# Square roots moved to GpSimd as powers, and pivots as ratios of a recurrence, in a two-layer graph network with an eigenvector chain

## The chip, the cores and the metric

The kernel runs on one core of one Trainium2 chip. The time is device microseconds for one execution; before the change it is 2428.49 us, the median of three runs (2427.74 to 2430.24). TensorE (PE) multiplies matrices, VectorE (DVE), ScalarE (ACT) and GpSimd (POOL) do elementwise work, and SyncE (SP) issues the transfers. Each engine runs its own instructions in order.

## The reference

The input is `x`, 64 batches of 256 nodes with 256 features, in float32, and one adjacency matrix `adj` of 256 x 256. Two layers follow each other, each behind a layer norm with a relu and a residual add:

```python
h = jnp.maximum(_layernorm(x, axis=-1), 0.0)
x = x + _L0_gnn_ref(h, adj, adj, W1, W2, W3)    # three graph convolutions, widths 512, 1024, 256
h = jnp.maximum(_layernorm(x, axis=-1), 0.0)
x = x + _L1_gnn_ref(h, adj, W1, b1, W2, b2)     # in the eigenvectors of a Laplacian
```

Layer 0 multiplies by `adj * adj` and by a weight three times in turn. Layer 1 builds the normalized Laplacian of `adj`, takes all its eigenvectors `U` (`jnp.linalg.eigh`), and computes `U relu(U^T h W1 + b1) W2 + b2` with them. So `U` depends on `adj` alone, but layer 1 can't begin without it.

## The kernel before

Two pieces of work run beside each other. The **chain** (class `Eigen`) finds the eigenvectors; it is sequential and mostly VectorE's. The **products** of layer 0 (class `Layers`) are TensorE's, 32 pairs of batches, with ScalarE emptying the PSUM banks. When the chain has ended, layer 1 runs over the 32 pairs (`layer1`, line 2107).

The chain has four stages. `laplacian` (402) makes the degrees, their roots (`root`, 349: a ScalarE square root, then one Newton step on VectorE) and the matrix. `tridiagonalize` (439) takes 254 Householder steps. In each, `length` (483) makes the squared length `nn` of the column and its root `s0`; the sign `q`, the products `qn`, `qs` and the reciprocal `rs` of the root make `nb` (513); `ac` follows from it, TensorE turns `ac` into a row (`psB`), and from there the next column `xn` and the updates of `A` (559 to 561). Small operations are on GpSimd (`aside`, 470) while the row number is below 128, and on VectorE after that; `alpha` and `none` are always on GpSimd. `leaves` (959) then solves 16 blocks of 16 at once, each block on eight partitions: `all_parts` (819) makes 32 steps, each of them a sequence of 15 pivots, one after the other:

```python
for k in range(w1):
    at, nxt = slice(k, k + 1), slice(k + 1, k + 2)
    self.recip(r[:, at], (q if k else asig)[:, at])
    self.stt(q[:, nxt], r[:, at], nba[:, at], asig[:, nxt], OP.mult, OP.add)
```

Between the pivots it puts operations left over from the step before (`behind`, from `turn_vectors`). Meanwhile `reflections` (583) builds the orthogonal matrix with TensorE. Last, `level` (1280) joins the blocks in four levels, with `rational_steps` (1189) for the roots of the secular equation (ScalarE roots of `rdq`, 24 in all) and roots `zh` and `rn` for the vectors. A flag `bad` is set when some test fails; then `mend` (1726) joins again with slower, safer methods.

The order of TensorE and ScalarE is written out by the planner `Pace` (161), and VectorE's, GpSimd's and SyncE's by the framework. For each operation of the chain `Pace.chain` works out when its inputs are due, by costs that it holds itself (`Op`, 83), and puts operations of layer 0 in front of it until then (`run`, 227). Its costs for the chain are multiplied by 1.06, in the blocks of 16 by 1.13. Two streams give it this filler: `products` (1849) and `rows` (1872), which makes the layer norms (`norm`, 1811) ahead of layer 0 and of layer 1, 64 in all. The last pair's turned rows and its product for layer 1 (1868 to 1870) are held until layer 1 has reached pass LAST_AT - 1 - 3 = 8. When the chain has ended, 3.5 us of filler cover the flag's reading (FLAG_US) and 4.5 us the first loads (LOAD_US). In `layer1` the planner puts about one filler operation before each of its own; at pass 8 `pace.finish()` puts out all that is left of layer 0 in one piece. Layer 1 takes the pairs in the order 0 to 10, 30, 31, 11 to 29; the last two pairs' inputs stay in SBUF, the others go through DRAM.

All of these calls pass through two helper lines, so the profile shows them as L209 (the planner's `issue`) or L213 (past `pace.finish`); tiles tell them apart. Tile names have their numbers cut off: `s` is `s0`, `m` is `nb`, `m1` and other matrices, `q` stands for all small vectors of `all_parts`, `psB` is the row of `ac`, `c` the columns `c0` to `c6`, `bank` every PSUM bank of the layers.

Of the kernel before, what the change touches and what calls it, by code (L numbers as in the profile page):

```python
# [21 lines left out]
F32 = mybir.dt.float32  # L22
AF = mybir.ActivationFunctionType
OP = mybir.AluOpType
# [58 lines left out]
class Op:  # L83
# [4 lines left out]
    def __init__(self, part, call, args, kwargs):  # L88
        self.part, self.engine, self.call, self.args, self.kwargs = part, ENGINES[part], call, args, kwargs
        self.name = call.__name__  # L90
        free = lambda a: int(np.prod([int(n) for n in a.shape[1:]]))
        named = dict(kwargs)
        outs = [named.pop("out")] if "out" in named else [args[0]]
        ins = [a for a in [*(args if "out" in kwargs else args[1:]), *named.values()] if isinstance(a, bass.AP)]
        total = named.pop("accum_out", None)
        if isinstance(total, bass.AP):
            outs.append(total)
            ins = [a for a in ins if a is not total]
        self.outs, self.ins = [span(a) for a in outs], [span(a) for a in ins]
        n = max(free(a) for a in outs[:1] + ins) if self.engine == "DVE" else free(outs[0])  # L100
        sums = len(outs) > 1

        if self.engine == "PE":
            self.columns = 0 if "transpose" in self.name else n
            self.busy = max(n * self.COLUMN, 0.224) if self.columns else 0.115
            self.until = max(self.busy, 0.165) + 0.35
        elif self.engine == "ACT":
            pointers = any(isinstance(kwargs.get(k), bass.AP) for k in ("scale", "bias"))
            self.busy = 0.13 + n / 1400 + 0.12 * pointers + 0.19 * sums
            self.until = self.busy + 0.12  # L110
        elif self.engine == "DVE":
            each = 6.3 if self.name == "reciprocal" else 2.0 if self.name == "tensor_tensor_scan" else 1.0
            pointers = self.name == "scalar_tensor_tensor" or any(a.shape[1:] == [1] for a in ins[1:])
            self.busy = 0.065 + 0.06 * pointers + each * n / 960 + 0.08 * sums
            self.until = self.busy + 0.125
        elif self.engine == "POOL":
            self.busy = 0.2 + 2 * n / 960
            self.until = self.busy + 0.1
        else:
            self.busy, self.until = 0.1, 4.0  # L120
# [160 lines left out]
class Eigen:  # L281


    def __init__(self, tc, ctx, ap, gt2, pace):
# [10 lines left out]
        self.load_matrices(0, 1)  # L295
        self.iota, self.far, self.ones = (pool.tile([P, N], F32, name=c) for c in ("iota", "far", "ones"))
        tc.nc.vector.memset(self.ones, 1.0)

        self.nc.scalar.activation(self.far[:, 0:1], self.ones[:, 0:1], AF.Sqrt)
        self.cols = pool.tile([P, 1 + len(LEVELS), H], F32, name="cols")  # L300
# [44 lines left out]

    def recip(self, out, a):
        return self.nc.vector.reciprocal(out, a)

    def root(self, out, a, tmp, scale=1.0):

# [51 lines left out]
    def laplacian(self):  # L402
# [11 lines left out]
        self.tt(deg, deg, t, OP.add)  # L414
        self.tt(deg, deg, dg, OP.subtract)

        safe, rt, tmp = self.col("c3"), self.col("c4"), self.col("c5")
        self.ts(safe, deg, 1e-30, OP.max)
        self.root(rt, safe, tmp)
        dinv = self.col("c6")  # L420
        self.recip(dinv, rt)
# [17 lines left out]
    def tridiagonalize(self, a):  # L439
# [22 lines left out]
            return ps  # L462

        row = lambda tag: self.sp.tile([P, N], F32, tag=tag, name=tag)
        guard = self.col("guard", 1)
        nc.vector.memset(guard, 1e-30)
        book = self.mat("m1")
        alphas, nbs, tails = book[:, 0, :], book[:, 1, :], self.mat("m2")[:, 0, :]

# [12 lines left out]

        def length(xr, lo, tail):

            nn, s0, q, qn = (self.col(c, 1) for c in ("nn", "s0", "q", "qn"))
            x1 = xr[:, lo : lo + 1]
            self.stt(nn, x1, x1, tail, OP.mult, OP.add)
            nc.scalar.activation(s0, nn, AF.Sqrt, bias=guard)
            aside(lo).tensor_scalar(q, x1, 0.0, 0.5, OP.is_ge, OP.subtract)
            aside(lo).tensor_tensor(qn, q, nn, OP.mult)  # L490
            return nn, s0, q, qn
# [6 lines left out]
        nn, s0, q, qn = length(xr, 1, tail)  # L498
        for k in range(N - 2):
            lo = k + 1  # L500
            r, rest = slice(lo, N), slice(lo + 1, N)
# [1 line left out]
            hs = slice(halves[0], H)  # L503
            rc = a[:, :, lo]

            rs, qs, nb = self.col("rs", 1), self.col("qs", 1), nbs[:, k : k + 1]
            self.recip(rs, s0)
            aside(lo).tensor_tensor(qs, q, s0, OP.mult)
            xa, junk = self.col("xa"), self.row("r0")
            for h in halves:  # L510
                self.stt(junk[:, r], a[:, h, r], 1.0, xr[:, r], OP.mult, OP.mult, accum=xa[:, h : h + 1])
                if h == halves[0]:
                    self.stt(nb, rs, qn, qs, OP.mult, OP.add)

            ac, uc = self.col("ac"), us[:, :, k]
            self.stt(ac[:, hs], rc[:, hs], nb, xa[:, hs], OP.mult, OP.add)
# [44 lines left out]
                self.stt(a[:, h, r], xr[:, r], wc[:, h : h + 1], a[:, h, r], OP.mult, OP.add)  # L561
            xr, xc = xn, xcn
            if more:
                alpha, tail, (nn, s0, q, qn) = alpha1, tail1, following

        done = slice(0, N - 2)
        e0 = self.row("r1")[:, done]
# [120 lines left out]
    def vec(self, tag, w=LEAF):  # L688
        return self.lp.tile([P, w], F32, tag=tag, name=tag)
# [129 lines left out]
    def all_parts(self, d, bb, es, z, pend, bad):  # L819
# [21 lines left out]
        ad, thr, df, q4, rt, m, adh, sg, st, ebs, den, ba, nba, sgr, asig = (vec() for _ in range(15))  # L841
        q, r, qi, t, gs, qq, x, s2, p = (vec() for _ in range(9))

        def couplings():

# [36 lines left out]
        for step in range(QL_QUICK):  # L882
# [62 lines left out]
        put_aside()  # L945
        left = self.lp.tile([P, 1], F32, tag="ln", name="left", bufs=2)
        nc.vector.tensor_reduce(left, act, AX.X, OP.add)
        self.tt(bad, bad, left, OP.add)
        self.tt(t, d, d, OP.mult)
        self.ts(t, t, 4.0, OP.is_le)  # L950
# [238 lines left out]
    def rational_steps(self, n, kd, zsum, zown, znxt, acc, s, gap, half, y, bs, rb):  # L1189
# [33 lines left out]
        for step in range(ROOT_STEPS):  # L1223
# [41 lines left out]
            nc.scalar.activation(dq, dq, AF.Sqrt)  # L1265
            self.tt(b, b, dq, OP.add)
            self.recip(b, b)
            self.tt(g, g, b, OP.mult)
# [11 lines left out]
    def level(self, n, qt, dc, rho, sg, bad=None):  # L1280
# [392 lines left out]
        self.recip(zp, zp)  # L1673
        self.root(zh, zp, tmp)
# [13 lines left out]
        self.root(rn, nrm, tmp)  # L1688
        self.recip(rn, rn)
# [43 lines left out]
class Layers:  # L1733


    def __init__(self, tc, ctx, ap, gt2, u, ut):
# [21 lines left out]
        self.b2 = pool.tile([P, N], F32, name="b2")  # L1758
        self.u1 = pool.tile([P, H], F32, name="u1")
        self.ub2 = pool.tile([P, H, N], F32, name="ub2")  # L1760

    def load_weights(self):
        dma, ap = self.nc.sync.dma_start, self.ap
# [47 lines left out]
    def norm(self, x, scale, shift, parts=range(4)):  # L1811

        nc = self.nc
        g = H * 2
        at = slice(parts[0], parts[-1] + 1, parts[1] - parts[0])
        s, nm, v, tmp = (self.sp.tile([P, g], F32, tag=c, name=c) for c in ("s", "nm", "v", "tmp"))
        for j in parts:
            junk = self.sp.tile([P, N], F32, tag="junk", name="junk", bufs=1)
            yield nc.scalar.activation(junk, x[:, j // 2, j % 2, :], AF.Copy, accum_out=s[:, j : j + 1])
        yield nc.vector.tensor_scalar(nm[:, at], s[:, at], -1.0 / N, None, OP.mult)  # L1820
        for j in parts:
            junk = self.sp.tile([P, N], F32, tag="junk", name="junk", bufs=1)
            yield nc.scalar.activation(
                junk, x[:, j // 2, j % 2, :], AF.Square, bias=nm[:, j : j + 1], accum_out=v[:, j : j + 1]
            )
        s, nm, v, tmp, scale, shift = (t[:, at] for t in (s, nm, v, tmp, scale, shift))
# [371 lines left out]
```

## Time and profile before

| | |
|---|---|
| median of the runs | 2428.49 us |
| span of the profiled execution | 2426.6 us |
| TensorE busy | 2381.5 us |
| VectorE busy | 2127.2 us |
| ScalarE busy | 1013.8 us |
| GpSimd busy | 480.6 us |
| mean granted clock of TensorE | 0.999 |
| the chain: steps of the tridiagonal stage end | 1325 us |
| blocks of 16 end, levels begin (about) | 1766 us |
| flag written | 2243.2 us |
| layer 1's products alone | from 2293 us |

The profiled execution's own time is its span; the median of the runs, which also counts what lies around the span, is 1.9 us longer. "Busy" counts an engine's instructions, overlaps once. A row of a group gives the busy time, the mean ns of one and the idle time before it with its cause. Each float32 matmul or transpose of the program appears as two records.

### The profile page before, as it was taken

What the parts mean: (1) busy time and instruction counts of PE and PEld (TensorE: products, weight loads), DVE (VectorE), ACT (ScalarE), POOL (GpSimd) and SP (SyncE); (2) the same over time, 40 slices, a digit from 0 to 9 for tenths busy, and PEclk for the clock granted to TensorE, in tenths of its full rate; (3) what the DMA queues carried; (4) which work ended last, traced back from release to release, by engine and by line L of the source; (5) the groups of instructions that cost most, each with busy time, mean ns of one, the idle gap of its engine ahead of it and who ended that gap; (6) DMA issues with size and microseconds to landing.
All of it is one profiled execution on the core that took longest, in us unless ns stands there. A gap on an engine that the chain in (4) does not pass through costs nothing. (4 is left out here: it accounts for less than half of the span.)

```text
span 2426.6 us, 38393 instructions
## 1 busy us (share of the span) xinstructions
PE 2381.5 (98%) x9226; PEld 1581.7 (65%) x9226; DVE 2127.2 (88%) x12971; ACT 1013.8 (42%) x2827; POOL 480.6 (20%) x1752
## 2 busy tenths in 40 slices
PE   7999999999999999999999899999999999999999
PEld 4666666666666566666666666666566666666788
DVE  8999999999999999999999989999997888886443
ACT  4444454444444444344444244344344434443322
POOL 2334333343333111111111000000000000000443
PEclk9999999999999999999999999999999999999999
DMA  3000000000000000000000000000000000000676
GB/s 113 18 21 7 23 23 18 23 23 23 6 23 23 18 22 23 22 6 23 23 23 26 10 23 23 23 23 22 18 22 27 22 23 12 16 22 1 210 255 204
DMA packets 59399, 90.02 MB, mean 37 GB/s; under 512 B 5792, under 2 KB 42784, under 8 KB 59168
## 3 DMA queue, kind: packets, MB, share of 16 engines
q1 hardware_dynamic: 59168, 87.52, 10.8%
q8 instruction: 74, 1.21, 0.2%
q14 instruction: 157, 1.29, 0.2%
HBM read 47.13 MB, written 40.37 MB: 36 GB/s over the span
## 5 line engine op out<-in xcount | busy, mean ns | idle before, releaser
L209 PE MATMUL bank<-y,L_gnn_W 128*128 128x512 f32 (+2 forms) x2182 | 903.5, 566 | 1.1 <-ACT y L209 1.1
L209 PEld LDWEIGHTS bank<-y,L_gnn_W 128*128 128x128 f32 x2182 | 401.8, 190 | 440.7 <-issue 419.0
L209 PE MATMUL bank<-L_gnn_W,s 128*128 128x256 f32 (+1 forms) x2092 | 465.2, 375 | 3.2 <-ACT s L209 3.2
L209 PEld LDWEIGHTS bank<-L_gnn_W,s 128*128 128x128 f32 x2092 | 386.7, 190 | 52.2 <-ACT s L209 3.9
L209 ACT ACTIVATE s<-bank 128x512 f32<-128x512 f32 x384 | 224.9, 586 | 196.4 <-PE bank L209 196.0
L209 PE MATMUL bank<-gt,s 128*128 128x256 f32 x1036 | 233.7, 379 | 2.8 <-ACT s L209 2.8
L209 PE MATMUL bank<-L_gnn_W,y 128*128 128x512 f32 (+2 forms) x542 | 230.9, 569 | 1.1 <-ACT y L209 1.1
L209 PEld LDWEIGHTS bank<-gt,s 128*128 128x128 f32 x1036 | 194.7, 191 | 39.7 <-issue 10.5
L209 ACT COPY y<-bank 128x512 f32<-128x512 f32 x192 | 111.5, 582 | 138.9 <-PE bank L209 138.6
L209 PEld LDWEIGHTS bank<-L_gnn_W,y 128*128 128x128 f32 x542 | 100.2, 190 | 97.3 <-issue 91.1
L209 POOL COPY m<-xr 128x1 f32<-128x1 f32 x254 | 55.8, 220 | 534.5 <-DVE xr L209 526.5
L209 ACT ACTIVATE s<-nn,guard 128x1 f32<-128x1 f32 x254 | 74.5, 293 | 208.1 <-DVE nn L209 169.0
L209 ACT ACTIVATE h<-x,shift,scale 128x256 f32<-128x256 f32 x256 | 137.3, 589 | 54.6 <-DVE shift L209 54.4
L209 ACT ACTIVATE junk<-x 128x256 f32<-128x256 f32 x256 | 105.6, 412 | 95.8 <-DVE x L209 80.5
L209 ACT ACTIVATE junk<-x,nm 128x256 f32<-128x256 f32 x256 | 129.0, 504 | 37.1 <-DVE nm L209 32.6
L209 DVE SCALAR_TENSOR_TENSOR A<-xr,wc,A 128x255 f32<-128x255 f32 (+63 forms) x381 | 139.9, 368 | 0.0
L209 DVE SCALAR_TENSOR_TENSOR A<-wr,q,A 128x255 f32<-128x255 f32 (+63 forms) x381 | 138.9, 366 | 0.0
L209 ACT ACTIVATE junk<-xr 128x254 f32<-128x254 f32 (+63 forms) x127 | 46.0, 362 | 216.5 <-DVE xr L209 211.4
L209 DVE SCALAR_TENSOR_TENSOR q<-q 128x1 f32<-128x1 f32 (+1 forms) x576 | 119.8, 208 | 13.0 <-ACT q L209 2.3
L209 PE MATMUL bank<-gt,h 128*128 128x256 f32 (+1 forms) x518 | 120.6, 382 | 0.1
L209 POOL TENSOR_TENSOR xb<-x,ub 128x512 f32<-128x512 f32 x16 | 19.9, 1271 | 495.5 <-DMA hw<-hw 485.6
L209 PE MATMUL bank<-p,gt 128*128 128x512 f32 (+2 forms) x270 | 117.0, 570 | 0.1
(615 smaller groups left out, 4306.2 us busy)
## 6 DMA issues: line engine op xcount, KB each, us to landing
x<-x SPq DMA_DIRECT2D x60, 512.0 KB, 3.6
x<-in_x_dram SPq DMA_DIRECT2D x64, 256.0 KB, 3.7
out_dram<-out SPq DMA_DIRECT2D x64, 256.0 KB, 2.2
hw<-hw SPq DMA_DIRECT2D x60, 256.0 KB, 2.7
L_gnn_W<-in_L_gnn_W_dram SPq DMA_DIRECT2D x1, 2048.0 KB, 10.9
L_gnn_W<-in_L_gnn_W_dram SPq DMA_DIRECT2D x1, 1024.0 KB, 13.5
L_gnn_W<-in_L_gnn_W_dram SPq DMA_DIRECT2D x1, 512.0 KB, 6.3
mask<-in_c_blk_dram SPq DMA_DIRECT2D x2, 256.0 KB, 3.1
```

The costliest lines, as they stand in the source:

```text
L209: return op.call(*op.args, **op.kwargs)
```

## The change

There are two parts.

*Roots by powers.* A new helper `power(out, a, y)` is one GpSimd `tensor_tensor` with the operation `pow` and a constant tile of 0.5 or -0.5. It takes the place of the root with its Newton step and reciprocal in `laplacian` (`dinv`) and `level` (`zh`, `rn`), and of ScalarE's root in `length` and in `rational_steps`. In `tridiagonalize`, `nb` becomes `2 q s0`, so `rs`, `qn` and `qs` fall away. The layer norms lose seven VectorE operations and a ScalarE root; ScalarE's first sum is scaled so that it gives the negative mean at once, and three GpSimd operations follow: variance, power, shift. Two kinds of root stay as they were: ScalarE's in the blocks of 16, and `root` in `leaves` and for `sq` in `level`. The planner gets a cost for a power: 0.2 + 0.14 n + 0.15 us for n columns.

*Pivots as ratios.* In `all_parts` a three-term recurrence of one instruction per pivot replaces the reciprocal and the multiply-add: each instruction works on two elements, the next term and the product that the one after it needs. The recurrence starts again after eight terms. All reciprocals are taken at once, and `r` and `q` are products of terms with them. The largest inverse of each of the 32 steps is kept, and one above 1e30 sets the flag.

```diff
+    def power(self, out, a, y):
+        return self.nc.gpsimd.tensor_tensor(out, a, self.powers[y][:, 0 : out.shape[-1]], OP.pow)
...
-            nc.scalar.activation(s0, nn, AF.Sqrt, bias=guard)
+            self.power(s0, nn, 0.5)
             aside(lo).tensor_scalar(q, x1, 0.0, 0.5, OP.is_ge, OP.subtract)
-            aside(lo).tensor_tensor(qn, q, nn, OP.mult)
...
-            self.recip(rs, s0)
-            aside(lo).tensor_tensor(qs, q, s0, OP.mult)
...
-                    self.stt(nb, rs, qn, qs, OP.mult, OP.add)
+                    self.stt(nb, q, 2.0, s0, OP.mult, OP.mult)
...
-            for k in range(w1):
-                at, nxt = slice(k, k + 1), slice(k + 1, k + 2)
-                self.recip(r[:, at], (q if k else asig)[:, at])
-                self.stt(q[:, nxt], r[:, at], nba[:, at], asig[:, nxt], OP.mult, OP.add)
-                if k == 0:
-                    nc.vector.tensor_copy(q[:, at], asig[:, at])
+            nc.vector.tensor_copy(chain[:, :, 1, 0:2], coef[:, :, 0 : LEAF : half].rearrange("p c s -> p s c"))
+            for k in range(1, LEAF):
+                part, at = k // half, k % half + 1
+                old = chain[:, (k - 1) // half, (k - 1) % half + 1, :]
+                out = over if k == half else chain[:, part, at, 0:2]
+                self.stt(out, coef[:, :, k], old[:, 0:1], old[:, 1:3], OP.mult, OP.add)
+                if k == half:
+                    self.recip(whole, old[:, 0:1])
+                    next(behind, None)
+                    self.tt(chain[:, part, at, 0:1], over[:, 0:1], whole, OP.mult)
...
+            self.recip(invs, chain[:, :, :, 0])
+            self.tt(split(r), chain[:, :, 0:half, 0], invs[:, :, 1:], OP.mult)
+            self.tt(split(q), chain[:, :, 1:, 0], invs[:, :, 0:half], OP.mult)
+            nc.vector.tensor_reduce(largest[:, step : step + 1], invs.rearrange("p s k -> p (s k)"), AX.X, OP.max, apply_absolute_value=True)
...
-            nc.scalar.activation(dq, dq, AF.Sqrt)
+            self.power(dq, dq, 0.5)
...
-        yield nc.vector.tensor_scalar(v, v, 0.25 / N, 0.25 * LN_EPS, OP.mult, OP.add)
-        yield nc.scalar.activation(s, v, AF.Sqrt)
-        yield nc.vector.reciprocal(tmp, s)
-        yield nc.vector.tensor_tensor(tmp, tmp, v, OP.mult)
-        yield nc.vector.tensor_tensor(s, s, tmp, OP.add)
-        yield nc.vector.reciprocal(scale, s)
-        yield nc.vector.tensor_tensor(shift, nm, scale, OP.mult)
+        yield nc.gpsimd.tensor_scalar(v, v, 1.0 / N, LN_EPS, OP.mult, OP.add)
+        yield nc.gpsimd.tensor_tensor(scale, v, self.rsqrt[:, 0 : scale.shape[-1]], OP.pow)
+        yield nc.gpsimd.tensor_tensor(shift, nm, scale, OP.mult)
```

More of the change, by code (lines that the diff above doesn't have):

```diff
@@ L116, in __init__ @@
         elif self.engine == "POOL":
-            self.busy = 0.2 + 2 * n / 960
+            power = OP.pow in args
+            self.busy = 0.2 + (0.14 * n + 0.15 if power else 2 * n / 960)
             self.until = self.busy + 0.1
@@ L297, in __init__ @@
         tc.nc.vector.memset(self.ones, 1.0)
+        self.powers = {0.5: pool.tile([P, H], F32, name="half"), -0.5: pool.tile([P, H], F32, name="less")}
+        for y, t in self.powers.items():
+            tc.nc.vector.memset(t, y)
         self.nc.scalar.activation(self.far[:, 0:1], self.ones[:, 0:1], AF.Sqrt)
@@ L415, in laplacian @@
         self.tt(deg, deg, dg, OP.subtract)
-        safe, rt, tmp = self.col("c3"), self.col("c4"), self.col("c5")
+        safe, dinv = self.col("c3"), self.col("c6")
         self.ts(safe, deg, 1e-30, OP.max)
-        self.root(rt, safe, tmp)
-        dinv = self.col("c6")
-        self.recip(dinv, rt)
+        self.power(dinv, safe, -0.5)
         self.stt(dinv, deg, 0.0, dinv, OP.is_gt, OP.mult)
@@ L464, in tridiagonalize @@
         row = lambda tag: self.sp.tile([P, N], F32, tag=tag, name=tag)
-        guard = self.col("guard", 1)
-        nc.vector.memset(guard, 1e-30)
         book = self.mat("m1")
@@ L483, in length @@
         def length(xr, lo, tail):
-            nn, s0, q, qn = (self.col(c, 1) for c in ("nn", "s0", "q", "qn"))
+            nn, s0, q = (self.col(c, 1) for c in ("nn", "s0", "q"))
             x1 = xr[:, lo : lo + 1]
             self.stt(nn, x1, x1, tail, OP.mult, OP.add)
-            nc.scalar.activation(s0, nn, AF.Sqrt, bias=guard)
+            self.power(s0, nn, 0.5)
             aside(lo).tensor_scalar(q, x1, 0.0, 0.5, OP.is_ge, OP.subtract)
-            aside(lo).tensor_tensor(qn, q, nn, OP.mult)
-            return nn, s0, q, qn
+            return nn, s0, q
         xc = self.col("xc")
@@ L497, in tridiagonalize @@
         alpha, tail = below(xr, 1)
-        nn, s0, q, qn = length(xr, 1, tail)
+        nn, s0, q = length(xr, 1, tail)
         for k in range(N - 2):
@@ L504, in tridiagonalize @@
             rc = a[:, :, lo]
-            rs, qs, nb = self.col("rs", 1), self.col("qs", 1), nbs[:, k : k + 1]
-            self.recip(rs, s0)
-            aside(lo).tensor_tensor(qs, q, s0, OP.mult)
+            nb = nbs[:, k : k + 1]
             xa, junk = self.col("xa"), self.row("r0")
@@ L563, in tridiagonalize @@
             if more:
-                alpha, tail, (nn, s0, q, qn) = alpha1, tail1, following
+                alpha, tail, (nn, s0, q) = alpha1, tail1, following
         done = slice(0, N - 2)
@@ L840, in all_parts @@
         nsm, act = nx[:, 1 : LEAF + 1], act_x[:, 0:LEAF]
-        ad, thr, df, q4, rt, m, adh, sg, st, ebs, den, ba, nba, sgr, asig = (vec() for _ in range(15))
-        q, r, qi, t, gs, qq, x, s2, p = (vec() for _ in range(9))
+        ad, thr, df, q4, rt, m, adh, sg, st, ebs, den, ba, sgr = (vec() for _ in range(13))
+        q, r, qi, t, gs, qq, x, p = (vec() for _ in range(8))
+        coef = self.lp.tile([P, 2, LEAF], F32, tag="coef", name="coef")
+        asig, nba = coef[:, 0, :], coef[:, 1, :]
+        half = LEAF // 2
+        chain = self.lp.tile([P, 2, half + 1, 3], F32, tag="chain", name="chain")
+        nc.vector.memset(chain, 0.0)
+        nc.vector.memset(chain[:, :, 0, 0], 1.0)
+        invs = self.lp.tile([P, 2, half + 1], F32, tag="invs", name="invs")
+        split = lambda v: v.rearrange("p (s k) -> p s k", s=2)
+        over, whole = vec(2), vec(1)
+        largest = self.lp.tile([P, QL_QUICK], F32, tag="largest", name="largest")
         def couplings():
@@ L901, in all_parts @@
             self.ts(nba, ba, -1.0, OP.mult)
-            for k in range(w1):
-                at, nxt = slice(k, k + 1), slice(k + 1, k + 2)
-                self.recip(r[:, at], (q if k else asig)[:, at])
-                self.stt(q[:, nxt], r[:, at], nba[:, at], asig[:, nxt], OP.mult, OP.add)
-                if k == 0:
-                    nc.vector.tensor_copy(q[:, at], asig[:, at])
+            nc.vector.tensor_copy(chain[:, :, 1, 0:2], coef[:, :, 0 : LEAF : half].rearrange("p c s -> p s c"))
[8 more added lines that the diff above has]
+                    self.tt(chain[:, part, at, 0:1], over[:, 0:1], whole, OP.mult)
+                if k == 1:
                     put_aside()
@@ L947, in all_parts @@
         nc.vector.tensor_reduce(left, act, AX.X, OP.add)
+        self.tt(bad, bad, left, OP.add)
+        self.ts(largest, largest, 1e30, OP.is_gt)
+        nc.vector.tensor_reduce(left, largest, AX.X, OP.add)
         self.tt(bad, bad, left, OP.add)
@@ L1264, in rational_steps @@
             self.ts(dq, dq, 1e-36, OP.max)
-            nc.scalar.activation(dq, dq, AF.Sqrt)
+            self.power(dq, dq, 0.5)
             self.tt(b, b, dq, OP.add)
@@ L1672, in level @@
         self.ts(zp, zp, 1e-30, OP.max, 1e30, OP.min)
-        self.recip(zp, zp)
-        self.root(zh, zp, tmp)
+        self.power(zh, zp, -0.5)
         self.ts(tmp, zsc, 0.0, OP.is_ge, 0.5, OP.subtract)
@@ L1687, in level @@
         rn = self.col("rn")
-        self.root(rn, nrm, tmp)
-        self.recip(rn, rn)
+        self.power(rn, nrm, -0.5)
         for h in range(H):
@@ L1760, in __init__ @@
         self.ub2 = pool.tile([P, H, N], F32, name="ub2")
+        self.rsqrt = pool.tile([P, 2 * H], F32, name="rsqrt")
+        self.nc.vector.memset(self.rsqrt, -0.5)
     def load_weights(self):
@@ L1815, in norm @@
         at = slice(parts[0], parts[-1] + 1, parts[1] - parts[0])
[L1816 to L1820, printed above, removed]
+        nm, v = (self.sp.tile([P, g], F32, tag=c, name=c) for c in ("nm", "v"))
         for j in parts:
@@ L1823, in norm @@
             yield nc.scalar.activation(
-                junk, x[:, j // 2, j % 2, :], AF.Square, bias=nm[:, j : j + 1], accum_out=v[:, j : j + 1]
+                junk, x[:, j // 2, j % 2, :], AF.Copy, scale=-1.0 / N, accum_out=nm[:, j : j + 1]
             )
-        s, nm, v, tmp, scale, shift = (t[:, at] for t in (s, nm, v, tmp, scale, shift))
-        yield nc.vector.tensor_scalar(v, v, 0.25 / N, 0.25 * LN_EPS, OP.mult, OP.add)
-        yield nc.scalar.activation(s, v, AF.Sqrt)
-        yield nc.vector.reciprocal(tmp, s)
-        yield nc.vector.tensor_tensor(tmp, tmp, v, OP.mult)
-        yield nc.vector.tensor_tensor(s, s, tmp, OP.add)
-        yield nc.vector.reciprocal(scale, s)
-        yield nc.vector.tensor_tensor(shift, nm, scale, OP.mult)
+        for j in parts:
+            junk = self.sp.tile([P, N], F32, tag="junk", name="junk", bufs=1)
+            yield nc.scalar.activation(
+                junk,
+                x[:, j // 2, j % 2, :],
+                AF.Square,
+                bias=nm[:, j : j + 1],
+                accum_out=v[:, j : j + 1],
+            )
+        nm, v, scale, shift = (t[:, at] for t in (nm, v, scale, shift))
+        yield nc.gpsimd.tensor_scalar(v, v, 1.0 / N, LN_EPS, OP.mult, OP.add)
+        yield nc.gpsimd.tensor_tensor(scale, v, self.rsqrt[:, 0 : scale.shape[-1]], OP.pow)
+        yield nc.gpsimd.tensor_tensor(shift, nm, scale, OP.mult)
     def relu_norm(self, x, scale, shift, h, parts=range(4)):
```

## The prediction

> **What bounds the kernel now.** I read the page first, then busy time by stage, then TensorE's waits.
>
> ```profile
> span 2426.6 us, 38393 instructions
> PE 2381.5 (98%) x9226; PEld 1581.7 (65%) x9226; DVE 2127.2 (88%) x12971; ACT 1013.8 (42%) x2827; POOL 480.6 (20%) x1752
> ```
>
> TensorE is idle for only 45 us. VectorE's 88% is the eigenvector chain, which runs beside it. The stage table (columns: length, then busy time of PE, PEld, DVE, ACT, POOL) says where the 45 lie:
>
> ```profile
> 0.00:18.00 18.00, 6.60 (x18) 4.50 (x18) 9.20 (x56) 8.56 (x24) 0.20 (x4) 1.00 0.91 307
> 18.00:760.00 742.00, 734.77 (x2919) 480.04 (x2920) 709.54 (x3656) 346.15 (x1047) 290.06 (x1124) 1.00 0.06 20
> 760.00:1325.00 565.00, 561.22 (x2178) 361.88 (x2177) 544.89 (x4270) 245.96 (x671) 103.21 (x527) 1.00 0.06 20
> 1325.00:1390.00 65.00, 55.82 (x279) 44.89 (x278) 58.79 (x377) 14.60 (x34) 0.45 (x2) 0.97 0.05 16
> 1390.00:1745.00 355.00, 350.11 (x1179) 215.12 (x1178) 322.62 (x2519) 145.72 (x421) 6.01 (x28) 1.00 0.07 22
> 1745.00:2243.00 498.00, 496.64 (x1847) 323.16 (x1847) 408.26 (x1988) 205.73 (x544) 0.75 (x3) 1.00 0.05 18
> 2243.00:2258.00 15.00, 12.37 (x46) 8.18 (x45) 5.03 (x9) 5.57 (x18) 4.87 (x4) 1.00 0.58 212
> ...
> 2290.00:2427.00 137.00, 131.95 (x618) 115.78 (x616) 52.36 (x76) 31.46 (x52) 57.52 (x46) 1.00 0.65 213
> ```
>
> TensorE's busy time short of each length: start 11.4, tridiagonal stage 7.2 + 3.8 (rows below and above 128), blocks of 16 with the reflections 9.2 + 4.9, levels 1.4, hand-over 2.6, end 5.0. No row offers more than some 10 us. The table of TensorE's waits (total us, times, longest) names them:
>
> ```profile
> PE psC L209 <- DVE c L209: 6.3, 1, 6.3
> PE psD L209 <- DVE q L209: 5.3, 5, 1.5
> ...
> PE psB L209 <- DVE xr L209: 3.9, 8, 1.0
> PE psD L209 <- DVE rb L209: 3.8, 2, 2.8
> PE psB L209 <- DVE ac L209: 3.2, 6, 1.1
> ```
>
> `c` is the start (the degrees' root), `psD` the reflections, `xr` and `ac` the 254 steps: TensorE waits for a step in 14 places, 7 us in all. The timeline at the hand-over shows why the chain's length is no longer the bound:
>
> ```profile
> 2242.66 3.27 PE L209 MATMUL bank<-L_gnn_W,s 128*128 128x256 f32 x14
> ...
> 2246.94 2.81 PE L209 MATMUL bank<-p,gt 128*128 128x512 f32 x6
> ...
> 2251.32 1.97 PE L209 MATMUL bank<-hw,u 128*128 128x256 f32 x8 [1.57 <-ACT junk L209]
> ...
> 2252.47 2.49 POOL L209 TENSOR_TENSOR xb<-x,ub 128x512 f32<-128x512 f32 x2 [485.62 <-DMA hw<-hw]
> ...
> 2253.99 0.99 DVE L209 TENSOR_SCALAR nm<-s 128x4 f32<-128x4 f32 x1
> ```
>
> Layer 0's last product ends at 2249.7, just after the chain's flag at 2243.2: chain and filler end together. A later chain leaves TensorE empty; an earlier one only moves layer-0 work behind it.
>
> **Tridiagonal stage.** TensorE works in order and the planner (`Pace`) has put filler ahead of each of the chain's transposes, so a step takes the longer of the planner's charge and VectorE's real time; where the real one is longer, TensorE idles. The planner's VectorE costs times 1.06 sum to 5.44 us for a step with 178 columns (the trace has 5.48 from one `ac` to the next at 500 us) and 4.21 with 79 columns (trace 4.20 at 1000 us): balanced. Removed are
>
> ```profile
> L209 DVE RECIPROCAL rs<-s 128x1 f32<-128x1 f32 x254 | 39.8, 157 | 1.1 <-ACT s L209 0.4
> ...
> L209 DVE RECIPROCAL q<-q 128x1 f32<-128x1 f32 x480 | 77.3, 161 | 10.3
> ```
>
> the first of these in every step (0.08 of issue beside other work), and `qn` and `qs`, on VectorE in the second half (about 0.08 each), on GpSimd in the first, where `nb` waits some 0.16 for `qs`. Planner: 0.072 x 1.06 = 0.08 less per step in the first half; in the second 0.216 less by sum, but then its latency loop (4.09, with the root at 0.59 + two hops) rules: 0.12 less. 127 x 0.08 + 127 x 0.1 = 23 us. Real: 5.48 - 0.08 - 0.16 = 5.24 and 4.20 - 0.16 = 4.04 (`nb` follows the reads of `A` by no more than the root lets it). The layer norms, 63 with seven VectorE operations each, go to three on GpSimd: the planner sheds 0.53 each, 42 of them here, 22 us. Their stalls go too (VectorE waits 25 us in all for ScalarE's sums and roots); a GpSimd `v` that waits for ScalarE's sum now holds up the chain's `gg`, `gu` and root behind it instead, about the same.
>
> **The power.** The trace has none. Low end 0.19 us (one-element GpSimd tensor_tensor), high end 1.27 (its longest, 512 columns). I take the planner's figure in the diff, 0.2 + 0.14 + 0.15 = 0.49 for one column: its plain figure 0.2 + 2n/960 gives 0.20 and 1.27 where the rows show
>
> ```profile
> L209 POOL TENSOR_TENSOR gg<-z 128x1 f32<-128x1 f32 x127 | 24.7, 195 | 150.4 <-DVE z L209 149.4 <-DVE nm L209 1.0
> L213 POOL TENSOR_TENSOR xb<-x,ub 128x512 f32<-128x512 f32 x48 | 60.0, 1272 | 68.1 <-issue 62.7 <-DVE out L213 5.4
> ```
>
> In the first half some 1.1 us of updates of `A` cover it; in the second only two updates and one product (0.65 us).
>
> The Trainium skill ("SBUF — State Buffer", section "SBUF: two separate sides") speaks against this change: GpSimd and a VectorE instruction with two SBUF inputs exclude each other, for the whole instruction that came first. The row above agrees for long ones: `nm`, 0.18 elsewhere, took 0.99 and ended when the two `xb` did. One-element GpSimd operations don't show it: from 100 to 646 us, 160 updates of `A` that ran against `none` or `xc` took 0.00 us more. By the rule each power would hold VectorE for up to 0.45: 254 x 0.3 = 76 us. By the row, nothing. I take the row for one column, and keep the rule as a rival.
>
> **Blocks of 16.** A pivot costs a reciprocal and an SCALAR_TENSOR_TENSOR in sequence, 0.455 us from pair to pair; afterwards one of 0.255, with the operations from behind in its shadow. From first reciprocal to last pivot now 7.05 us; afterwards 0.2 (copy) + 15 x 0.255 + 0.4 (restart) + 0.3 (18 inverses) + 0.25 (two products, maximum) = 5.0. 32 x 2.05 = 66 us; by the planner 32 x 1.13 x (6.72 - 4.87) = 67. So the filler shrinks with it and TensorE doesn't starve.
>
> **Levels and start.** 24 roots of `rdq`: ScalarE 0.20, but 1.3 with its queue (26.9 us in 20 waits); GpSimd 0.63 + hops. The planner charges 0.5 more each, the trace would give 0.5 less: 0. The eight root sequences shed some 0.6 each: 5. `dinv` comes 1 us sooner, and TensorE waits for it (6.3 us for `c`): -1. ScalarE sheds 254 + 63 roots; it bounds nothing.
>
> **Where 115 us of shorter chain go.** 23 + 22 + 66 + 5: the flag comes near 2130, with 115 + 11 us of layer 0 left. Layer 1's planner lets about one filler matmul in front of each of its operations: twelve for its matmuls and, while it waits for the add, the relu, the copies and the stores, some eight more; 140 for the 7 pairs before pass 8. A pair of layer 0 has 124 TensorE operations in about 62 us (2381 us less 165 for layer 1 and some 230 of the chain's own, by 32), 0.5 each: with LOAD_US about 75 us. `pace.finish()` then puts out the other 50 us in one piece, ending with pair 31, and nothing may pass its layer norm: last add 0.7, two sums 1.1, four squares 2.5, three GpSimd operations 1.5, four relus 2.1, less 0.4, and about 1 for copies: 8.5 us of empty TensorE. Before, this norm lay under layer 1's first pairs.
>
> Sum: 2426.6 + 8.5 - 1 (start) - 2 (hand-over now filled) = 2432.1. The median is 1.9 above the profiled span: **2434.0**. The waits in the middle (26.5 us) can move by 8 either way: own range 2426 to 2442.
>
> **Rivals.** (a) *No tail*: the chain gains under 65 us, or more slips in; norm hidden: 2425.5. For it: real steps near the planner's; against: the pivots alone are 66. (b) *Faster*: the waits in the middle halve as VectorE is freed of norms, tail hidden: 2428.5 - 3 - 11 = 2415. Against: they come from the order, not from VectorE's sum. (c) *The power is long or holds the port*: in the second half the planner's average step is 4.06, the real one about 3.96; from 0.1 us more per step TensorE idles. At 0.4: 0.3 x 128 + 0.1 x 127 = 51 us, tail gone: 2478. For it: the port row; against: the one-element rows. (d) The new test of the inverses (1e30) sets the flag and the repair runs: more than the 910 us from 1331 to 2243 on top. Eight pivots of size 0.01 give 1e16, so unlikely.
>
> **Chances.** Likeliest 0.42, (a) 0.16, (b) 0.10, (c) 0.30, (d) 0.02. This kernel's measurement tells 0.2% (4.9 us) from nothing. Faster: (b) and a quarter of (a), 0.14; same: the rest of (a) and some 0.12 of the likeliest, 0.24; slower 0.62. The range 2420 to 2485 leaves out most of (b), (c)'s upper third and (d).
>
> **What would show it.** Right: flag near 2130; SCALAR_TENSOR_TENSOR on the chain 255 ns apart; one gap of about 8 us in TensorE after the last `x` add. Wrong: waits of TensorE for `ac` of over 10 us, A-updates lengthened beside powers (c); powers over 0.6 us; no gap (a).

## The result, and the profile after

The changed kernel takes 2442.75 us (median; 2441.29 to 2445.26), the kernel before, measured beside it, 2428.58 us. The ratio is 1.006, 95% interval 1.0048 to 1.0072: slower by 0.6%. The prediction was 2434.0, slower, with a range of 2420 to 2485; the likeliest case's own range ended at 2442, just short of the result.

The head of the page after:

```profile
span 2443.5 us, 36658 instructions
PE 2386.3 (98%) x9208; PEld 1582.1 (65%) x9208; DVE 1968.0 (81%) x11682; ACT 942.6 (39%) x2475; POOL 675.2 (28%) x1980
```

VectorE has lost 159 us of work and ScalarE 71, and the time went up. The span grew by 16.9 us: TensorE is idle 12.1 us longer (57.2 against 45.1) and busy 4.8 us longer. The stage table (length, then busy time of PE, PEld, DVE, ACT, POOL, then the granted clock, the DMA share and GB/s) says where. Its rows are the start, the steps of the upper and of the lower half, the reflections, the blocks of 16, the levels, the hand-over to layer 1, layer 1 with filler, the end of the filler, and layer 1 alone:

```profile
0.00:18.00 18.00, 6.31 (x18) 4.29 (x18) 7.80 (x47) 8.59 (x24) 2.33 (x9) 1.00 0.90 302
18.00:745.00 727.00, 716.81 (x2876) 473.30 (x2877) 683.03 (x3394) 303.65 (x871) 326.12 (x1062) 1.00 0.06 19
745.00:1303.00 558.00, 543.99 (x2103) 348.48 (x2102) 476.98 (x3679) 204.02 (x501) 192.88 (x687) 1.00 0.06 20
1303.00:1365.00 62.00, 56.96 (x213) 34.63 (x212) 54.38 (x350) 24.43 (x68) 5.84 (x17) 0.94 0.08 25
1365.00:1675.00 310.00, 308.46 (x1100) 198.47 (x1099) 288.71 (x2308) 121.29 (x336) 18.05 (x54) 1.00 0.06 20
1675.00:2170.00 495.00, 492.23 (x1782) 313.57 (x1781) 386.83 (x1808) 210.11 (x543) 47.41 (x82) 1.00 0.07 22
2170.00:2185.00 15.00, 14.85 (x65) 11.05 (x64) 2.16 (x6) 3.67 (x7) 4.08 (x4) 1.00 0.60 197
2185.00:2294.00 109.00, 109.00 (x433) 78.65 (x432) 14.73 (x22) 28.81 (x59) 17.11 (x16) 1.00 0.24 85
2294.00:2312.00 18.00, 10.23 (x39) 7.83 (x38) 1.38 (x3) 8.17 (x23) 6.30 (x7) 0.72 0.00 1
2312.00:2443.00 131.00, 127.41 (x591) 111.82 (x589) 52.00 (x76) 29.80 (x49) 55.08 (x44) 1.00 0.66 219
```

TensorE's idle time in each row (its length less the busy time), before in brackets: the steps 10.2 (7.2) and 14.0 (3.8), so 13.2 us more; the new row at 2294 7.8, beside a clock of 0.72; the reflections 5.0 (9.2), the blocks 1.5 (4.9) and the hand-over 0.15 (2.6), so 10 us less. There are two losses, at two ends of the program. The table of TensorE's waits (total us, times, longest) names both:

```profile
PE psB L210 <- DVE xr L210: 17.9, 23, 1.5
PE bank L210 <- ACT h L210: 7.8, 3, 6.7
PE psC L210 <- DVE c L210: 6.9, 1, 6.9
...
PE psB L210 <- DVE ac L210: 2.8, 5, 1.2
```

`xr` and `ac`, the steps, are 20.7 us in 28 waits (7.1 in 14 before). `h` comes from the layer norm of pair 31, which no other work of TensorE covers any more; below it is called the bare norm.

**The steps.** One step of the lower half, from the timeline after (start, duration, engine, instruction, and in brackets the idle time before it):

```profile
1003.43 0.21 DVE L210 SCALAR_TENSOR_TENSOR nn<-xr,m 128x1 f32<-128x1 f32 x1
...
1003.63 0.29 DVE L210 SCALAR_TENSOR_TENSOR A<-wr,q,A 128x76 f32<-128x76 f32 x1
1003.76 0.60 POOL L210 TENSOR_TENSOR s<-nn,half 128x1 f32<-128x1 f32 x1
...
1004.39 0.16 DVE L210 SCALAR_TENSOR_TENSOR m<-q,s 128x1 f32<-128x1 f32 x1 [0.46 <-POOL s L210]
1004.46 0.29 DVE L210 SCALAR_TENSOR_TENSOR A<-xr,wc,A 128x76 f32<-128x76 f32 x1
...
1005.15 0.22 DVE L210 SCALAR_TENSOR_TENSOR ac<-A,m,xa 128x1 f32<-128x1 f32 x1
```

The power takes 0.60 us, and `nb` (`m`) stands in VectorE's queue ahead of the second update of `A`. VectorE waits 0.46 us for the power with that update, and everything else, behind the waiting instruction. The same place in the kernel before:

```profile
1002.67 0.21 DVE L209 SCALAR_TENSOR_TENSOR nn<-xr,m 128x1 f32<-128x1 f32 x1
...
1002.88 0.29 DVE L209 SCALAR_TENSOR_TENSOR A<-wr,q,A 128x80 f32<-128x80 f32 x1
...
1003.21 0.30 DVE L209 SCALAR_TENSOR_TENSOR A<-xr,wc,A 128x80 f32<-128x80 f32 x1
...
1003.71 0.22 DVE L209 SCALAR_TENSOR_TENSOR m<-rs,qn,qs 128x1 f32<-128x1 f32 x1
1003.96 0.22 DVE L209 SCALAR_TENSOR_TENSOR ac<-A,m,xa 128x1 f32<-128x1 f32 x1
```

There both updates come ahead of `nb`, and this order, with two updates and a product as cover, is the one that the prediction counted on. It is also the order of the program's text, in both kernels; the framework moved `nb` forward. Why it did is not shown. The groups of the whole program (busy us, mean ns of one, idle before):

```profile
L210 POOL TENSOR_TENSOR s<-nn,half 128x1 f32<-128x1 f32 x254 | 162.8, 641 | 19.9
L210 DVE SCALAR_TENSOR_TENSOR A<-xr,wc,A 128x255 f32<-128x255 f32 (+63 forms) x381 | 139.7, 368 | 0.0
L210 DVE SCALAR_TENSOR_TENSOR A<-wr,q,A 128x255 f32<-128x255 f32 (+63 forms) x381 | 138.4, 365 | 0.0
```

641 ns, against the planner's 490 and the 293 of ScalarE's root before. The mean mixes two cases: 21 powers with no VectorE instruction beside them took 0.56 us, those of the lower half 0.59 in the mean, those of the upper half, beside longer updates of `A`, 0.69 and up to 0.98 (spans on GpSimd are rough). The updates of `A` take 368 and 365 ns, and took 368 and 366 before. In the table of VectorE's waits:

```profile
DVE m L210 <- POOL s L210: 84.2, 153, 2.1
```

Between 760 and 1310 us, in the lower half, are 121 of these waits, with 67.4 us.

**The tail.** TensorE and its suppliers at the end of layer 0, from the timeline after:

```profile
2291.74 3.68 PE L210 MATMUL bank<-p,gt 128*128 128x512 f32 x8
...
2295.46 0.69 DVE L210 TENSOR_TENSOR x<-x,bank 128x512 f32<-128x512 f32 x1 [1.03 <-PE bank L210]
...
2299.91 0.19 POOL L210 TENSOR_SCALAR v<-v 128x4 f32<-128x4 f32 x1 [37.56 <-ACT junk L210]
2300.19 1.01 POOL L210 TENSOR_TENSOR scale<-v,rsqrt 128x4 f32<-128x4 f32 x1
2301.28 0.20 POOL L210 TENSOR_TENSOR shift<-nm,scale 128x4 f32<-128x4 f32 x1
...
2302.16 0.47 PE L210 MATMUL bank<-eye,h 128*128 128x128 f32 x1 [6.74 <-ACT h L210]
```

From its last matmul to the first relu's result TensorE has nothing: 6.74 us, and another 1.0 in two waits of 0.5, for the next relu and for a copy. What follows runs slowly. The same columns as in the stage table, in stretches of 2 us:

```profile
2300.00:2302.00 2.00, 0.00 (x0) 0.00 (x0) 0.00 (x0) 0.49 (x1) 1.84 (x4) 0.53 0.00 0
2302.00:2304.00 2.00, 1.33 (x5) 0.83 (x6) 0.00 (x0) 1.59 (x4) 2.00 (x3) 0.50 0.00 0
2304.00:2306.00 2.00, 1.48 (x7) 1.08 (x6) 0.00 (x0) 1.07 (x2) 2.00 (x2) 0.50 0.00 0
2306.00:2308.00 2.00, 2.00 (x11) 2.00 (x10) 0.00 (x0) 0.00 (x0) 0.37 (x1) 0.50 0.03 8
2308.00:2310.00 2.00, 2.00 (x10) 1.82 (x9) 0.00 (x0) 0.59 (x1) 0.00 (x0) 0.50 0.00 0
2310.00:2312.00 2.00, 2.00 (x10) 1.74 (x9) 0.26 (x1) 0.00 (x0) 0.00 (x0) 0.91 0.00 0
```

The granted clock falls to half in the gap, at 2300, and stays there until about 2310, 8 us after TensorE began again. The busy times at half clock, 1.33, 1.48, 2.00 and 2.00, sum to 6.8 us, so about 3.5 us of work are lost on top of the gap.

**The chain.** Its marks, from the timelines: the first `ac`, the last one of two columns (upper half), the last one, the last test `bad<-bad,left` of the blocks, and the start of the instruction that writes the flag.

| | before | after | difference of the stage |
|---|---|---|---|
| first `ac` | 21.9 | 21.3 | -0.6 |
| upper half ends | 769.3 | 752.5 | -16.2 |
| lower half ends | 1322.3 | 1310.9 | +5.4 |
| blocks end | 1756.4 | 1679.2 | -65.8 |
| flag | 2243.0 | 2170.0 | +4.2 |

The flag comes 73 us earlier, not 113. The pivots gave what was forecast for them. One instruction per pivot, from the timeline after:

```profile
1388.69 0.22 DVE L210 SCALAR_TENSOR_TENSOR chain<-coef,chain 128x2 f32<-128x2 f32 x1
...
1388.95 1.25 DVE L210 SCALAR_TENSOR_TENSOR chain<-coef,chain 128x2 f32<-128x2 f32 x5
1390.23 0.27 DVE L210 RECIPROCAL invs<-chain 128x18 f32<-128x18 f32 x1
```

Five in 1.25 us and 0.26 from the one ahead of them: the 255 ns of the prediction.

### The profile page after: what moved, and what is told of

It reads as the page before. It is cut to its first block, busy times and chain, and to the rows that moved or that the text cites. A ratio compares the mean times of both kernels' runs of the same rounds, so it can differ in the third digit from the quotient of the medians.

```text
span 2443.5 us, 36658 instructions
## 1 busy us (share of the span) xinstructions
PE 2386.3 (98%) x9208; PEld 1582.1 (65%) x9208; DVE 1968.0 (81%) x11682; ACT 942.6 (39%) x2475; POOL 675.2 (28%) x1980
## 5 line engine op out<-in xcount | busy, mean ns | idle before, releaser
L210 PE MATMUL bank<-y,L_gnn_W 128*128 128x512 f32 (+3 forms) x2178 | 911.7, 568 | 0.5 <-DVE x L210 0.5
L210 PE MATMUL bank<-L_gnn_W,s 128*128 128x256 f32 x2086 | 466.6, 375 | 0.0
L210 PE MATMUL bank<-gt,s 128*128 128x256 f32 (+1 forms) x1040 | 233.6, 376 | 0.9 <-ACT s L210 0.7
L210 POOL TENSOR_TENSOR s<-nn,half 128x1 f32<-128x1 f32 x254 | 162.8, 641 | 19.9
L210 ACT COPY p<-bank 128x512 f32<-128x512 f32 x64 | 37.3, 583 | 257.2 <-PE bank L210 257.2
L210 DVE SCALAR_TENSOR_TENSOR r<-A,xr 128x255 f32<-128x255 f32 (+63 forms) x381 | 117.6, 309 | 0.1
## 6 DMA issues: line engine op xcount, KB each, us to landing
L_gnn_W<-in_L_gnn_W_dram SPq DMA_DIRECT2D x1, 2048.0 KB, 11.1
```

Source lines behind the costliest of these rows:

```text
L210: return op.call(*op.args, **op.kwargs)
```

## Experiments

The theory after the result: the loss is (i) the steps' waits, because the power takes longer than the planner counts and `nb` waits for it in VectorE's order, some 13 us, and (ii) the bare norm with the half clock behind it, some 12. The two together are more than the 14.2 lost, since other waits got shorter. The rivals: the port between GpSimd and VectorE; a cost of the pivots; a cost of all powers alike. Intervals of ratios are at 95%. "Before" was 2429.14 us beside the first four runs, 2428.31 beside the next four, 2428.01 beside the next three and 2428.93 beside the last.

### The pivots alone, and the roots alone

The kernel before with the new `all_parts`, and the changed kernel with the old one:

```diff
-                self.recip(r[:, at], (q if k else asig)[:, at])
-                self.stt(q[:, nxt], r[:, at], nba[:, at], asig[:, nxt], OP.mult, OP.add)
...
+                self.stt(out, coef[:, :, k], old[:, 0:1], old[:, 1:3], OP.mult, OP.add)
```

This is the core of the first against the kernel before; the second undoes the same lines in the changed kernel.

> Only the pivots of the blocks of 16 are changed; roots and layer norms stay as before. My theory (two costs: TensorE waits for the steps because the power is longer than the planner's charge, 13 us; the layer norm of pair 31 lies bare after pass 8, 7.8 us idle and about 5 us at half the granted clock): the chain ends 66 us sooner, flag near 2177 us, no waits for the steps beyond the 7 us of before. Some 77 us of layer 0 are left, at the edge of what passes 0 to 7 take in: 2423 if the norm is still hidden, 2435 if it lies bare. Rival (any shorter chain gains, TensorE has room): 2415 or less. Rival (the shorter chain is worth nothing and costs nothing): 2428.

> Only the roots and the layer norms are changed; the pivots stay as before. My theory: the chain is about as long as before (17 us sooner in the upper half of the steps, 4 in the lower, 14 later in the levels: flag 2236), so pair 31's norm is hidden as before, and the waits of TensorE for the steps (13 us more) remain: 2438 to 2441. Rival (the whole loss is the bare norm): 2427. Rival (powers hold the port of VectorE): VectorE's updates of A are longer than 365 to 368 ns in the mean, and the time is above 2445.

Pivots alone: 2424.64 us (2422.12 to 2427.39), ratio 0.9981 (0.9974 to 0.9988). Roots alone: 2442.62 us (2439.28 to 2443.06), ratio 1.0053 (1.0037 to 1.007). The two parts are of opposite sign, and the roots make the change slow. The pivots alone bring the flag to 2178.4, 65 us earlier, and still no norm stands bare: TensorE waits 1.5 us for `h` in two waits. The steps are as before, `xr` and `ac` 7.8 us. The roots alone, just above the forecast, have the steps' waits in full, with the flag at 2235.7 and no bare norm; their updates of `A` take 369 and 366 ns, so a port held by the powers does not show:

```profile
PE psB L210 <- DVE xr L210: 18.1, 25, 1.5
...
PE psB L210 <- DVE ac L210: 3.0, 4, 1.2
```

-4.5 and +13.5 add up to +9.0, and both together are +14.2. The remaining 5 us come with what only the two together do, which is to lay the norm bare: a chain shorter by 73 us does, and one shorter by 65 or by 7 does not.

### The last pair later

The last pair's turned rows and product are held until pass LAST_AT - 4; with 16 the planner has four more passes of layer 1 to spread filler over.

```diff
-LAST_AT = 12
+LAST_AT = 16
```

> The changed kernel with LAST_AT 16 instead of 12: what is left of layer 0 is put out at pass 12, so four more passes can take it in. My theory: the gap of 7 us in TensorE after the last add of x goes, and with it the stretch at half clock: 2430, the waits for the steps stay at 17 us. Rival (the gap only moves: the norm of pair 31 lies bare wherever layer 0 ends): 2442.

2434.02 us (2430.82 to 2435.24), ratio 1.0019 (1.001 to 1.0027). The flag stands where it was (2170.8) and the steps wait as before (18.0 and 2.9 us), but the tail is full. The stretch of the gap, in the stage table's columns:

```profile
2294.00:2312.00 18.00, 18.00 (x78) 14.56 (x77) 7.15 (x11) 9.73 (x26) 8.74 (x9) 1.00 0.51 175
```

18.00 busy at clock 1.00 where the changed kernel has 10.23 at 0.72. The edit takes 8.7 us off the median, where 13 were expected. TensorE's waits for `h` fell from 7.8 us to 0.6, and its busy time from 2386.3 to 2382.1, about what the half clock had cost. The kernel before has nothing to gain from this:

> The kernel before with LAST_AT 16, the control for the three runs with it. If a later pass helps only where much filler is left at the flag, 2428.5 +- 2 (in this kernel 3.3 us of filler stood behind the flag's first 6 us). If it gives the same 3.4 us as with the pivots alone, 2425.

2427.61 us, ratio 0.9996 (0.9988 to 1.0004): no difference. Nor do the pivots gain enough from it to be told:

> Pivots alone, with LAST_AT 16. With 12 no bare norm was seen, so if the late passes only cost where the norm stands bare, nothing moves: 2424.6 +- 1.5. If some of the filler's piece at pass 8 costs time there too (TensorE's idle time in the tail), up to 4 us less: 2420.5.

2421.19 us, ratio 0.9973 (0.9962 to 0.9984), against 0.9981 (0.9974 to 0.9988) with 12: the point values differ by some 3 us, the intervals overlap. No norm stood bare there, so up to 3 of the 8.7 us above may be something else that later passes save; this is not shown either way.

### The planner told the power's length

```diff
-            self.busy = 0.2 + (0.14 * n + 0.15 if power else 2 * n / 960)
+            self.busy = 0.2 + (0.15 * n + 0.25 if power else 2 * n / 960)
```

> The changed kernel with the planner's charge for a power set to what the profile shows: 0.45 + 0.15 n us instead of 0.35 + 0.14 n (one column 0.60, four 1.05). My theory: the planner puts more filler in each step of the lower half, so TensorE's waits for xr and ac fall from 20 to under 8 us; the chain ends later, flag near 2180 to 2190, and with less of layer 0 left the norm may be hidden: 2432 if only the waits go, 2420 if the gap goes too. Rival (the waits come from something else than the charge): 2441 to 2444.

2430.67 us (2427.26 to 2432.58), ratio 1.0007 (0.9998 to 1.0016). VectorE still waits for the power (77.0 us in 154 waits), but the planner now puts more filler in front of the transposes:

```profile
PE psB L210 <- DVE xr L210: 11.5, 17, 1.5
...
PE psB L210 <- DVE ac L210: 4.1, 5, 1.5
```

15.6 us in place of 20.7; the lower half's empty time falls from 14.0 to 8.3. That is twice what was expected to remain. The flag moves to 2178.5, eight us later than in the changed kernel, and with that the norm is hidden again (1.3 us for `h`). So this run takes away both costs in part, and it does not measure the first alone.

The dearer charge helps, but the changed kernel's own figures show that the power's length is not the main error. By `Op` and `issue`, with the factor 1.06, `nb` can start 1.01 us after `nn` starts (0.27 for `nn`, 0.06, 0.62 for the power, 0.06), and `ac` 0.27 after that. In the lower half of the changed kernel's trace the means are 1.06 and 0.74; in the kernel before the second was 0.26. What the planner does not have is the second update of `A` and the rest behind the wait: `issue` lets VectorE go on for WINDOW = 1.0 us past an instruction that waits.

With both edits:

> The changed kernel with both repairs: LAST_AT 16 and the planner's power charge at 0.2 + 0.15 n + 0.25. If the two costs are separate, their gains over the changed kernel add up: 8.7 + 12.1 = 21, so 2422 us, slightly faster than the kernel before. If the dearer charge alone already hid the norm (there the layer norm of pair 31 did not stand bare), the second repair adds nothing: 2430.

2427.35 us, ratio 0.9996 (0.9987 to 1.0004): not the sum, and nearer to the second forecast. Once the chain is longer the norm is hidden anyway.

### The root of `length` back on ScalarE

```diff
-            self.power(s0, nn, 0.5)
+            nc.scalar.activation(s0, nn, AF.Sqrt)
```

> The changed kernel with ScalarE's root back in `length` alone; `nb` stays 2 q s0, and all other powers stay. Theory (the power takes 0.64 us where the planner counts 0.49, and `nb` waits for it in VectorE's order): TensorE's waits for `xr` and `ac` fall from 20.7 us to below 8; the bare norm at the end stays; some 2442.8 - 13 = 2430 us. Rival (the waits come from the planner's smaller charge for a step without `rs`, `qn` and `qs`, whoever makes the root): waits stay at 18 or more, 2440 to 2443. Third possibility: VectorE's wait for the root stays as long because ScalarE has a queue in front of it, waits of 8 to 18.

2425.89 us (2423.74 to 2428.42), ratio 0.9991 (0.9984 to 0.9997): 17 us less than the changed kernel by one line. The root is also shorter than in the kernel before (201 ns, 293 there), as it has no `guard` tile. `nb` is still 2 q s0 and still stands ahead of the second update, but the root is there in time. The same place in a step, from this run's timeline:

```profile
1000.34 0.28 DVE L210 SCALAR_TENSOR_TENSOR A<-wr,q,A 128x71 f32<-128x71 f32 x1
1000.45 0.20 ACT L210 ACTIVATE s<-nn 128x1 f32<-128x1 f32 x1 [4.03 <-DVE nn L210]
...
1000.68 0.16 DVE L210 SCALAR_TENSOR_TENSOR m<-q,s 128x1 f32<-128x1 f32 x1
1000.76 0.28 DVE L210 SCALAR_TENSOR_TENSOR A<-xr,wc,A 128x71 f32<-128x71 f32 x1
```

VectorE waits 0.7 us for this root in the whole program (84.2 for the power), so the third possibility, a queue on ScalarE, did not come. TensorE waits 9.7 us for `xr` and `ac`, somewhat more than forecast. The rival by which the shorter charge of a step makes the waits, whoever makes the root, would have left 18 or more. The lower half takes 519 us (558 with the power, 553 before) and the flag comes at 2122: the power had cost the chain 48 us, 39 of them in these 127 steps. The bare norm is still there (7.8 us for `h`). The gain is 4 us more than the forecast 13: in the spans, 11.1 us of it are TensorE's idle time, and 7.1 its busy time (2379.2 us in place of 2386.3), which was not forecast and stays open. Then the same with a later last pair, at 16 and, in the second run, at 22:

```diff
-LAST_AT = 12
+LAST_AT = 22
...
-            self.power(s0, nn, 0.5)
+            nc.scalar.activation(s0, nn, AF.Sqrt)
```

> The changed kernel with ScalarE's root back in `length`, and LAST_AT 16. If the steps' waits and the bare norm are the whole loss, both go: 2442.8 - 13 - 9 = 2421 us, TensorE's waits for `xr` and `ac` below 8 and no gap before the last pair's product. If other powers (levels, layer norms) cost something of their own, it stays above 2427.

> The changed kernel with ScalarE's root back in `length`, and LAST_AT 22 in place of 16: with 16 there still were 4 us of empty TensorE and a granted clock of 0.66 over 10 us. More passes take more filler, so the piece at the end becomes small and the norm of pair 31 is hidden: 2421.8 - 3 - 3 = 2415.5 us. If the gap isn't the norm's but that of layer 1's first products, it stays: 2421.

With 16: 2421.77 us, ratio 0.9971 (0.9961 to 0.9981), as forecast, but still 4.3 us of waits for `h`, with a clock of 0.58 and 0.74 in the two stretches of 5 us from 2300. With 22: **2413.65 us** (2412.11 to 2414.72), ratio 0.9942 (0.9928 to 0.9956), the fastest of all, and the tail is closed:

```profile
2290.00:2300.00 10.00, 10.00 (x48) 8.81 (x47) 4.26 (x7) 7.28 (x20) 5.24 (x7) 1.00 0.47 165
2300.00:2310.00 10.00, 10.00 (x48) 8.79 (x48) 4.13 (x6) 2.43 (x4) 6.03 (x5) 1.00 0.79 255
```

### The roots of the levels back on ScalarE

```diff
-            self.power(dq, dq, 0.5)
+            nc.scalar.activation(dq, dq, AF.Sqrt)
```

This is done at both places in `rational_steps`; everything else is the changed kernel's.

> The changed kernel with ScalarE's roots back for `rdq` alone (24 in the levels). Theory: the levels are paced by the planner, which charges a power of two columns 0.73 us to its end, a root on ScalarE less; the 14 us that the levels grew from before (477 to 491) are this charge. Then levels of 478 +- 4 us and the flag some 12 us earlier, near 2158; TensorE's work is the same, so the filler only moves into layer 1, the bare norm stays: 2441 to 2447. Rival (the real durations of the power or its hops lengthen the levels): levels stay at 488 or more and the flag near 2170.

2445.73 us, ratio 1.0073 (1.0059 to 1.0087; the changed kernel 1.0048 to 1.0072). The levels take 479.3 us from the blocks' last test to the flag (490.8 with powers; 486.6 before, where the expectation's 477 starts from a rougher mark), and the flag comes at 2157.1. That is 11.5 us for 24 roots, 0.48 each: near the planner's charge, and hardly the powers' real length, since VectorE waits longer for `rdq` here (32.3 us in 24 waits) than for the powers (20.7). The chain is 13 us shorter and the kernel no faster.

### What the other roots are worth

> Pivots alone with LAST_AT 22, to tell what the roots other than `length`'s are worth (against 2413.7 us with them, ScalarE's root in `length` and the same LAST_AT). With 16 no gap of the norm was left here, so 22 should do nothing more: 2421 us, and the roots' part (layer norms on GpSimd, `nb` from one product, the start) is then worth 7. If the late pass itself brings the 7 us, 2415.

2421.89 us, ratio 0.9972 (0.9961 to 0.9982): as with LAST_AT 16. Between it and the 2413.65 above, whose interval lies apart, stand the layer norms on GpSimd, `nb` from one product, the powers of the start and the levels, and ScalarE's root without its `guard` tile: together 8 us. In the two profiles TensorE's idle time is the same (39.6 and 39.8 us) and its busy time is 9.0 us shorter with them. About 2.5 of the 9.0 are the clock: with them it is 1.00 in every stretch of 10 us, and in the pivots' run it is 0.83 in the stretches from 1340 and from 1610 and 0.96 from 2410, each behind a gap or at the end. Which matmuls make the rest I could not tell from the records, because the groups overlap in time; that stays open.

## Why the prediction was right or wrong

- **The total: inside the range, in part by luck.** The forecast's +5.5 us came from the tail alone, with nothing for the steps. In the spans the steps are +13.2 and the tail with its half clock some 11, and the likeliest case's own range was missed; the wide range that rival (c) asked for holds the result. Of the prediction's own signs, the 255 ns and the one gap came, the flag near 2130 did not, and "powers over 0.6 us" pointed to (c).
- **The bound and the direction: right**, though with the tail filled the kernel was still slower (1.0019), for a reason that the likeliest case had not. TensorE's order decides. A chain shorter by 65, 73, 121 or 125 us gave 2424.6, 2442.8, 2425.9 and 2413.7 us, so its length alone says nothing.
- **The pivots, 66 us: right**, 65.8 measured, and the filler shrank with them.
- **Where the chain's gain goes: right.** The filler left at the flag is the chain's gain and the 11 us there were. The capacity of "about 75 us" in layer 1's first passes lies between the runs: at 65 + 11 = 76 us left (pivots alone) the norm is hidden, at 73 + 11 = 84 it is bare. Rival (a), "no tail" with a gain under 65 us, came true in that run, at 2424.6 against its 2425.5.
- **The bare norm, 8.5 us: right in place, short in price.** 7.8 us of empty TensorE were measured. The half clock after it, about 3.5 us, was missing in the sum. Here the Trainium skill should have been weighed: "TensorE: Matmul & The Clock Gate", section "Part 1: The HAM clock gate (the 'warmup' mystery)", says that about 3.4 us of idleness bring TensorE to half clock until it has been busy as long again; from that one would estimate 1.7 us of lost work. This trace agrees on the half (0.50), but it lasted 8 us of resumed work, of which the first 3 were broken by two waits of 0.5. In the kernel before a gap of 2.8 us at 1342, shorter than the page's, was followed by half clock too.
- **The power, 0.49 us: too small.** It took 0.59 us in the lower half (641 ns over all 254), 697 ns with two columns, 1.04 us with four.
- **The steps, "4.20 - 0.16 = 4.04" and 23 us saved: this step failed**, in the lower half. It took the order of the kernel before for granted, in which two updates of `A` stand ahead of `nb`. After the change one stands there, and VectorE waits for the power in 153 steps, 121 of them well inside the lower half. From one `ac` to the next a lower step got shorter by 0.025 us (the median, step against step) where 0.16 was forecast (in the mean, which takes in other work on VectorE between, it got 0.04 longer); with ScalarE's root it got shorter by 0.32. The reading of 4.20 was short too: the steps before around 1000 us take 4.27, from `ac` at 999.69 to 1003.96, already 0.06 over the planner's 4.21. The lower half grew by 5.4 us where 13 less were forecast; the upper half, where GpSimd takes other small work, shed 16.2, norms included, where 10 and its share of the norms' 22 were forecast. TensorE waited 13.2 us more, as rival (c) has it "from 0.1 us more per step", while the likeliest case had nothing there. ScalarE's root in its place, one line, brought TensorE's waits for `xr` and `ac` from 20.7 to 9.7 us.
- **The port: right to leave out, for VectorE.** The updates of `A` did not lengthen by 1 ns in the mean. In the upper half, 68 products `r<-A,xr` of two inputs started inside a power, with 0.58 us of it still to run in the mean; they took 0.377 us, 0.372 for the same widths before. It is the powers that are longer beside them (0.69 against 0.56 us with nothing beside). `nm`, with which the prediction backed the rule for long operations, has a single tensor input, so it is no case of the rule as quoted. Rival (c) was half right: the power is long, but what it holds up is VectorE's order.
- **The levels, 0 and -5: half right.** The 24 roots cost the chain 11.5 us by the planner's charge; as the levels grew only 4.2, the rest shed 7.3. The real durations, by which I had offset the charge, have no say where the planner puts filler ahead.
- **The start, -1: not seen**, +0.3; TensorE waits 6.9 us for `c`, 6.3 before, and 5.3 to 7.8 over the runs. **The hand-over, -2: right**, -2.5.
- **Not forecast:** 7.5 us less idle time in the reflections and the blocks; its cause was not tested.

The sum with what was measured: steps +13.2, tail +7.8, busy time +4.8 (3.8 of it clock below full), hand-over -2.5, reflections and blocks -7.5, the start, the levels and the end together +1.1 (0.3, 1.4 and -0.6), is 16.9, as the spans differ. The forecast had 5.5.

## What to carry to other kernels

Moving a short operation to an idle engine was decided here by its latency at the place where its result is awaited in order, not by the busy time that it frees: look at what the order has between the operation and its consumer after the change, not before. Where a planner fills the bounding engine, shortening the chain beside it can pay only as long as there is cover for the filler that is left over; the same pivots that gained 0.2% alone laid a norm bare together with the roots. And price a gap on TensorE with the slow clock that comes after it.

## What the runs showed of the hardware

- A gap of TensorE of 6.7 us was followed by a granted clock of 0.50 for 8 us of resumed work, 10 us with the end of the gap; the same in the run with ScalarE's root in `length` (6.7 us, then 0.50 and 0.80 over two stretches of 5 us). Shorter gaps were enough: after 2.8 and 2.4 us in the kernel before (ending at 1344.7 and 1715.6) and 2.8 us in the pivots' run (1617.4) the clock was 0.50 for some 3.4 us each, and after 3.1 us, with two waits of 0.5 to 0.7 behind it, for 6.8 us (0.58 and 0.74 over two stretches of 5 us).
- A GpSimd power costs 641 and 697 ns for one and two columns of 128 rows in the mean (two others of two columns took 0.86 us) and 1041 for four, against 201 ns for a ScalarE square root of one column without a bias tile and 293 with one. With one column it is 0.56 us with no VectorE instruction beside it and up to 0.98 beside VectorE's updates.
- Powers on one column do not slow VectorE's two-input instructions that run beside them (updates of `A` 368 ns before and after; products that start inside a power 0.377 us, 0.372 before).
